# Transposing W_base and the first batch's x1 by 32x32 blocks and a trip through DRAM

## The chip, the cores and the metric

The kernel runs on one core of a Trainium2 chip. The metric is the device time of one execution in microseconds, as the median of several runs. A profiled execution has its own time and its own span, from the first to the last instruction.

The engines are named as in the profile: PE (TensorE, matmuls, with PEld for its weight loads), DVE (VectorE), ACT (ScalarE), POOL (GpSimd) and SP (SyncE, which issues nearly all DMAs here). Each engine works through its own queue in order, and an instruction that waits holds up everything behind it on that engine. That holds for SP too: a DMA that has to wait for data keeps the DMAs behind it from being issued.

## The reference

One transformer layer in float32, with normalisation after each half:

```python
x = layernorm(x + attention(x))        # x: (2, 512, 512)
x = layernorm(x + ffn(x))
```

The attention has 32 query heads over 8 key/value heads of 128, rotary positions and a causal mask. The second half is a linear layer with a low-rank addition, mixed over four experts:

```python
y        = einsum('bth,oh->bto', x, W_base) + b_base      # W_base: (512, 512), o by h
z        = einsum('bth,erh->bter', x, A)                  # A, Bm: 4 active experts of rank 8
contribs = einsum('bter,eor->bteo', z, Bm) * 2.0
alpha    = softmax(log(prior + 1e-12) + (x @ router_W.T + router_b)[..., active])
return y + einsum('bteo,bte->bto', contribs, alpha)
```

Both operands of the first product are contracted over h. TensorE contracts over partitions, so it needs the normalised tokens and W_base with h on the partitions, and both arrive with h along the free dimension. They have to be transposed.

## The kernel before

**Tiles.** The 2 x 512 tokens are eight tiles of 128 tokens, four for each batch (TPB = 4). `x_sb` holds them; the attention's output is added into it, so after the attention it holds x + attention(x). A unit is one key/value head group of one batch; there are 16 units (NU), in four parts each (one part = 128 queries of four heads), so 64 parts.

**Slots.** The middle of the kernel is a hand-written pipeline: `slot(T)` for T from -8 to E + 6, with E = T_END = 256. One slot computes one block of scores (`sc`, 32 queries of four heads). Their masked maximum and exponentials follow in the next slot, and three and four slots later come their normalisation and their 32x32 block transposes. Extra work is put into a slot with `put(slot, f)`; it comes last in that slot's order, in the order of the `put` calls. `A = LAST + LAG_WO` is slot 245, by which the output projection of the first batch has been added, and `T_PROJ` is slot 237.

**The probabilities' way through DRAM.** For `weigh` (`pc<-pT,v`) the probabilities must be transposed as well. VectorE transposes 32x32 blocks into `zt`; `blocks_out` writes them to DRAM (`db`) in four DMAs, one from each group of 32 partitions; `blocks_in` reads them back as `pT` with the blocks in their places. `blocks_out` comes in slots with T % 4 = 3 and `blocks_in` in slots with T % 4 = 1, one part at a time. Both are on the SP queue, as are the loads of wq, wk, wv and wo.

**The first batch's second half.** Its four tiles are `f0`. Each is an `Ffn` object with the steps `stats`, `centre` (normalise in place), `transpose` (four TensorE transposes into PSUM, one ScalarE copy to `xT`, named x1T in the profile), `base` (the main product, eight matmuls of 272 or 276 columns, half of them in each of two slots), `logits`, `alphas`, `low_rank`, `finish` and `add`. They are laid into the slots from A on, while the last parts of the attention of the second batch still run. The `po<-wo,ctxT` matmuls in those slots are its output projection. The second batch's tiles (`fa`, `fb`, `fc`) come after the slots, in plain order.

**W_base.** Four loads of 128 rows are put into slots T_PROJ + 0, 1, 4 and 5. `transposed_base(c)` in slots T_PROJ + 3, 6, 8 and 9 transposes one of them: four TensorE transposes into a bank of PSUM and a ScalarE copy into `wbT`.

**Memory.** The pools open and close in a stack. `late` is a small pool that lives from slot 20 to T_PROJ; it holds `wt_late`, which is used by one set of output weights from slot 197 on. `ffn_pool` opens at T_PROJ in place of the projections' pool. The program's DMAs on the SP queue use eight completion semaphores ("lanes") in turn; a DMA that takes a lane waits until the DMA that had it before has landed, unless that is already known.

Of the kernel before, what the change touches and what calls it, by code (L numbers as in the profile page):

```python
# [9 lines left out]
F32 = mybir.dt.float32  # L10
# [5 lines left out]
P = 128  # L16
# [13 lines left out]
def postln_layer_kernel(  # L30
# [33 lines left out]
    nc = tc.nc  # L64
    B, S, HID = x.shape
    NT = B * S // P
    TPB = S // P
    KC = HID // P
    E_TOT, RK, _ = lora_A.shape
    O = W_base.shape[0]  # L70
    OC = O // P
# [4 lines left out]
    BLK = 32  # L76
    QB = P // BLK
    UNIT = S // BLK
# [17 lines left out]
    def set_units(n):  # L96
        return [u for u in range(NU) if set_of(u) == n]
# [9 lines left out]
    ps_k = ctx.enter_context(tc.tile_pool(name="ps_k", bufs=1, space=bass.MemoryType.PSUM))  # L107
# [3 lines left out]
    dram = ctx.enter_context(tc.tile_pool(name="dram", bufs=2, space=bass.MemoryType.DRAM))  # L111
# [42 lines left out]
    def load_q(n, k):  # L154
        wq_g = wts.tile([P, KC, 2 * D], F32, tag="wq_g", name=f"wq_{n}_{k}", bufs=3)
        lo = (sets[n] * R + 2 * k) * D
        nc.sync.dma_start(out=wq_g, in_=Wq[:, lo : lo + 2 * D].rearrange("(c p) n -> p c n", p=P))
        wqk["q", n, k] = wq_g
# [16 lines left out]
    for n in range(2):  # L175
# [6 lines left out]
        out=tri, in_=tri, pattern=[[-BLK, QB], [-1, BLK]], compare_op=ALU.is_ge,  # L182
# [98 lines left out]
    def transpose_token_tile(dst, src, pool, tag, copy, chunks=range(KC)):  # L281

        tp = pool.tile([P, len(chunks), P], F32, tag=tag, name="tp")
        for n, c in enumerate(chunks):
            nc.tensor.transpose(tp[:, n, :], src[:, ts(c, P)], ident)  # L285
        copy(dst[:, chunks[0] : chunks[-1] + 1, :], tp)

    b_jar = setup.tile([P, BJ, EA, RK], F32, name="b_jar")

# [340 lines left out]
    wt = {}  # L630
# [3 lines left out]
    def wo_block(n, c_half, n_half):  # L634
        return wos[n][:, CH * c_half : CH * (c_half + 1), ts(n_half, NHALF)]

    def wo_sums(n, step):

        if step == 0:
            shape = [P, 3, CH, NHALF]  # L640
            if n == NSETS - 4:
                wt[n] = late["pool"].tile(shape, F32, name="wt_late")
            else:
                wt[n] = wow.tile(shape, F32, tag="wt", name=f"wt_{n}", bufs=1)
        t1, t2, t4 = (wt[n][:, m] for m in range(3))
        b11, b12, b21, b22 = (wo_block(n, c_half, n_half) for c_half in range(2) for n_half in range(2))
        nc.vector.tensor_tensor(
            *((t1, b12, b11), (t2, b22, t1), (b12, b22, b12), (t4, b21, t2))[step], ALU.subtract)
# [104 lines left out]
    class Ffn:  # L753
# [22 lines left out]
        def transpose(self, pool, tag):  # L776
            transpose_token_tile(self.xT, self.x, pool, tag, nc.scalar.copy)
# [107 lines left out]
    def put(slot, f):  # L885
        extra.setdefault(slot, []).append(f)
# [21 lines left out]
    def q_from(u, k):  # L908

        return UNIT * u - 25 + 8 * k  # L910

    pairs = [(n, k) for n in range(NSETS) for k in range(R // 2)]
    for m, (n, k) in enumerate(pairs):
        if n:
            put(q_from(set_units(n)[0], k) - (5 if n == 1 else 9), lambda n=n, k=k: w_sums(n, k))
        if m > 3:
            before, k_before = pairs[m - 3]
            put(q_from(set_units(before)[-1], k_before) + 10, lambda n=n, k=k: load_q(n, k))


    PLAIN_K = 2 * B
    KV_FROM = 8
    late = {}
    PERIOD = VG * B * UNIT
    for p in range(1, G // VG):
        at = PERIOD * p
# [22 lines left out]
    for n in range(NSETS - 2):  # L949
        at = {0: (-5, -4, -3, -2), NSETS - 4: (-16, -15, -15, -13), NSETS - 3: (-11, -9, -6, -5)}.get(n, (0, 1, 1, 3))  # L950
        for k in range(4):
            put(wo_from(set_units(n)[0]) + at[k], lambda n=n, k=k: wo_sums(n, k))
# [98 lines left out]
    for t in range(TPB):  # L1051
        x_to = xT[:, :, ts(t, P)], x_sb[:, t, :]
        if t > 1:
            for c in range(KC):
                k_tile(0, t - 2, c)
        if t < TPB - 1:
            transpose_token_tile(*x_to, *spare[t], copies[t % 2])
        else:
            for n, bank in enumerate((spare[t], (ps_q, "qx"))):
                transpose_token_tile(*x_to, *bank, copies[n], range(2 * n, 2 * n + 2))  # L1060
        if t == 2:
            tb = ps_sc.tile([P, NBIAS], F32, tag="sc", name="tb")
            nc.tensor.transpose(tb, bqk, ident[:NBIAS, :NBIAS])
            nc.vector.tensor_copy(bqkT, tb)
# [63 lines left out]
    T_PROJ = T_END - 19  # L1128
# [1 line left out]
        slot(T)  # L1130
    proj_stack.close()
    ffn_pool = ctx.enter_context(tc.tile_pool(name="ffn", bufs=1))
    wb_sb = ffn_pool.tile([P, OC, HID], F32, name="wb_sb")
    wbT = ffn_pool.tile([P, KC, 2, WX_COLS], F32, name="wbT")
    nc.gpsimd.tensor_copy(wbT[:, :, 0, OH : OH + ARH], arT[:, :, :ARH])
    nc.gpsimd.tensor_copy(wbT[:, :, 1, OH:], arT[:, :, ARH:])
# [5 lines left out]
    QX, QY, SC, CTX = (ps_q, "qx"), (ps_q, "qy"), (ps_sc, "sc"), (ps_ctx, "ctx")  # L1142

    def tiles(ts_, banks, name):
        n = len(ts_)
        norms = Norm(ffn_pool, n, f"a{name}"), Norm(ffn_pool, n, f"f{name}")
        return [Ffn(t, bank, *norms, i) for i, (t, bank) in enumerate(zip(ts_, banks))]

    f0 = tiles(range(TPB), ((QX, QY), (QX, QY), (SC, SC), (QX, QY)), "0")
    fa = tiles([TPB + i for i in order[:2]], ((SC, SC), (WX, WY)), "1a")  # L1150
    (fb,) = tiles([TPB + order[2]], ((QX, QY),), "1b")
# [2 lines left out]
    A = LAST + LAG_WO  # L1154

    def transposed_base(c):
        transpose_token_tile(wbT[:, :, c // 2, ts(c % 2, P)], wb_sb[:, c, :], ps_k, "k", nc.scalar.copy)

    for c in range(OC):
        put(T_PROJ + (0, 1, 4, 5)[c], lambda c=c: nc.sync.dma_start(out=wb_sb[:, c, :], in_=W_base[ts(c, P), :]))  # L1160
        put(T_PROJ + (3, 6, 8, 9)[c], lambda c=c: transposed_base(c))
    put(A - 5, lambda: f0[0].norm1.newton(0, 2))
    for k, f in enumerate(f0):
        put(A + (-7, -6, 0, 0)[k], f.stats)
        if k == TPB - 1:
            put(A, lambda: f0[0].norm1.newton(2, TPB))
        put(A + 1 + k // 2, f.centre)
        put(A + 3 + k // 2, lambda f=f, k=k: f.transpose(*(QX, QY)[k % 2]))
    for f, at in zip(f0, (A + 5, A + 11, A + 13)):
        last = f is f0[2]  # L1170
        for c in range(KC):
            put(at + c // 2, lambda f=f, c=c: f.base(c))
        put(at + 2, lambda f=f: (f.logits(), f.alphas()))
        put(at + 3 + last, f.low_rank)
        if not last:
            put(at + 4, lambda f=f: (f.finish(), f.add()))
# [143 lines left out]
```

## Time and profile before

| | |
|---|---|
| Median of 3 runs | 817.26 us (816.86 to 817.88) |
| The profiled execution: its time / its span | 816.9 us / 815.1 us |
| Granted TensorE clock, mean | 0.998 |
| PE busy | 807.0 us, 3457 matmuls |
| DVE busy | 609.8 us, 1978 instructions |
| ACT busy | 384.9 us, 1074 instructions |
| POOL busy | 338.6 us, 392 instructions |
| Moved by DMA | 116.00 MB, mean 142 GB/s |

The profile's times count from the first instruction of the profiled execution. Each row of a timeline has a start, a length, an engine, the line of the program, the operation, what it writes and reads, and how many instructions it merges. A length includes a pipeline's latency, so that neighbouring rows overlap; the cost of a group of matmuls is read from start to start. Every float32 matmul of the program is two MATMUL records in the profile. Rows of waits give the waiting engine and line, what ended the wait, the total, how often, and the longest.

### The profile page before, as it was taken

To read this page: it belongs to the slowest core of one execution; us is meant where nothing else is said; L and a number is where in the kernel's file an instruction comes from. 1 tells how busy PE (TensorE), PEld (TensorE's weight loads), DVE (VectorE), ACT (ScalarE), POOL (GpSimd) and SP (SyncE) were. 2 spreads that over 40 slices of the span, in tenths; PEclk is the share of its full clock that TensorE was granted. 3 is DMA by queue.
4 is the path that set the end of the run, shared out by engine and by line. 5 is a ranking of instruction groups with operands and counts; after the bars stand their busy time and mean duration, and the time that the engine had idled before them with its cause. 6 is when DMAs were issued, how large, how long until landed. Compare 5 with 4: busy or idle time off the path is not lost.

```text
span 815.1 us, 11389 instructions
## 1 busy us (share of the span) xinstructions
PE 807.0 (99%) x3457; PEld 609.7 (75%) x3457; DVE 609.8 (75%) x1978; ACT 384.9 (47%) x1074; POOL 338.6 (42%) x392
## 2 busy tenths in 40 slices
PE   9999999999999999999999999999999999999996
PEld 7887777777777778777777778777777878656575
DVE  4778877687879886787867876787888689973455
ACT  2355454444545454545435454544545454663244
POOL 8666645421444345322443245343464333420033
PEclk9999999999999999999999999999999999999999
DMA  9025736355455637264544637365453726674211
GB/s 298 26 72 143 219 83 202 91 130 156 134 169 136 182 93 219 77 181 129 147 147 121 178 82 219 91 160 179 137 146 91 232 66 181 189 263 143 77 39 65
DMA packets 84415, 116.00 MB, mean 142 GB/s; under 512 B 6525, under 2 KB 64237, under 8 KB 82306
## 3 DMA queue, kind: packets, MB, share of 16 engines
q1 hardware_dynamic: 83154, 114.71, 49.0%
q8 instruction: 27, 0.44, 0.2%
q10 hardware_dynamic: 752, 0.42, 0.2%
q14 instruction: 34, 0.28, 0.1%
q0 software_dynamic: 448, 0.14, 0.1%
HBM read 71.21 MB, written 44.04 MB: 141 GB/s over the span
## 4 chain that ended last, share of the span: by engine, by line
PE 96%; POOL 1%; DVE 1%; ACT 1%; issue 0%; POOLq 0%
PE pc L618 17%; PE sc L562 15%; PE qx L450 14%; PE wx L450 12%; PE qy L450 10%; PE wy L450 9%; PE kx L450 4%; PE vx L528 4%; PE po L694 3%; PE py L788 3%; PE pv L348 3%; PE pp L365 1%; PE tp L285 1%; PE py L829 1%; POOL zt L191 0%; POOL act_er L220 0%
## 5 line engine op out<-in xcount | busy, mean ns | idle before, releaser
L577 ACT ACTIVATE p<-sc,nmax 128x288 f32<-128x288 f32 (+15 forms) x256 | 124.2, 485 | 197.7 <-DVE nmax L570 175.2
L570 DVE CUSTOM_DVE_ANT_0 sc<-sc,maskw 128x288 f32<-128x288 f32 (+15 forms) x256 | 114.2, 446 | 136.3 <-PE sc L562 134.7
L618 PE MATMUL pc<-pT,v 128*128 128x512 f32 x320 | 165.3, 599 | 0.0
L562 PE MATMUL sc<-kT,qT 128*128 128x160 f32 (+15 forms) x512 | 161.7, 398 | 0.3 <-ACT p L577 0.3
L386 POOL TENSOR_TENSOR qT<-q,t 128x512 f32<-128x512 f32 x64 | 88.0, 1376 | 176.1 <-DVE q L385 165.0
L585 ACT ACTIVATE p<-p,den 128x288 f32<-128x288 f32 (+15 forms) x256 | 133.2, 521 | 0.0
L562 PEld LDWEIGHTS sc<-kT,qT 128*128 128x128 f32 x512 | 96.1, 190 | 21.9 <-issue 8.1
L625 ACT ACTIVATE ctxT<-pc,bqkT 128x512 f32<-128x512 f32 x64 | 44.0, 688 | 114.8 <-PE pc L618 114.7
L437 POOL TENSOR_TENSOR cs<-ctxT 128x256 f32<-128x256 f32 x28 | 22.4, 801 | 158.5 <-PE wy L450 95.4
L593 DVE STREAM_TRANSPOSE zt<-p 128x128 f32<-128x128 f32 (+2 forms) x192 | 81.7, 426 | 0.0
L486 ACT COPY q<-qx 128x256 f32<-128x256 f32 x128 | 47.4, 370 | 51.4 <-PE qx L450 49.8
L618 PEld LDWEIGHTS pc<-pT,v 128*128 128x128 f32 x320 | 57.1, 190 | 18.7 <-issue 5.7
L450 PE MATMUL qx<-xs,wq 128*128 128x256 f32 x256 | 66.3, 381 | 0.0
L450 PEld LDWEIGHTS qx<-xs,wq 128*128 128x128 f32 x256 | 47.3, 190 | 23.2 <-issue 18.4
L595 DVE STREAM_TRANSPOSE zt<-p 128x32 f32<-128x32 f32 (+3 forms) x256 | 57.6, 225 | 0.0
L450 PE MATMUL wx<-wo,ctxT 128*128 128x256 f32 x224 | 57.5, 379 | 0.0
L378 DVE SCALAR_TENSOR_TENSOR t<-q,bqkT,rope_sb 64x512 f32<-64x512 f32 x64 | 52.3, 818 | 3.5 <-ACT q L486 1.7
L381 DVE SCALAR_TENSOR_TENSOR t<-q,bqkT,rope_sb 64x512 f32<-64x512 f32 x64 | 50.3, 786 | 1.5
L577 ACT ACTIVATION_READ_ACCUMULATOR p<-sc,nmax 128x1 f32 x256 | 49.8, 194 | 0.0
L385 DVE SCALAR_TENSOR_TENSOR q<-q,bqkT,rope_sb 128x512 f32<-128x512 f32 x64 | 48.1, 751 | 0.1
L450 PEld LDWEIGHTS wx<-wo,ctxT 128*128 128x128 f32 x224 | 42.5, 190 | 7.0 <-issue 1.4
L680 DVE TENSOR_TENSOR x_sb<-wx,x_sb 128x256 f32<-128x256 f32 x112 | 47.0, 420 | 0.0
(234 smaller groups left out, 1468.3 us busy)
## 6 DMA issues: line engine op xcount, KB each, us to landing
db<-zt SPq DMA_DIRECT2D x64, 256.0 KB, 4.3
pT<-db SPq DMA_DIRECT2D x16, 1024.0 KB, 4.8
db<-zt SPq DMA_DIRECT2D x64, 192.0 KB, 3.3
pT<-db SPq DMA_DIRECT2D x16, 768.0 KB, 4.4
wq<-in_L_attn_Wq_dram SPq DMA_DIRECT2D x20, 512.0 KB, 5.1
wo<-in_L_attn_Wo_dram SPq DMA_DIRECT2D x10, 1024.0 KB, 9.0
db<-zt SPq DMA_DIRECT2D x64, 128.0 KB, 2.4
pT<-db SPq DMA_DIRECT2D x16, 512.0 KB, 4.2
```

Of the source, the lines that this page charges most:

```text
L378: nc.vector.scalar_tensor_tensor(t2[lo, :], q[hi, :], b_ap[hi, :], rope_sb[hi, 1, :], ALU.add, ALU.mult)
L381: nc.vector.scalar_tensor_tensor(t2[hi, :], q[lo, :], b_ap[lo, :], rope_sb[lo, 1, :], ALU.add, ALU.mult)
L385: nc.vector.scalar_tensor_tensor(t1, q, b_ap, rope_sb[:, 0, :], ALU.add, ALU.mult)
L386: nc.gpsimd.tensor_tensor(dst, t1[:, :].rearrange("p (n s) -> p n s", s=BLK), t2[:, :].rearrange("p (n s) -> p n s", s=BLK), ALU.add)
L450: nc.tensor.matmul(ps, lhsT=wt[:, c, :], rhs=xt[:, c, :], start=start and c == 0, stop=c == CH - 1, skip_group_check=True)
L562: nc.tensor.matmul(sc[s][:, :w], lhsT=qT[u][:, i * QB + n].rearrange("p r s -> p (r s)"), rhs=kT[u][:].rearrange("p n s -> p (n s)")[:, :w ...
L570: nc.vector.tensor_tensor_reduce(sc[s][:, :w], sc[s][:, :w], maskw[:, S - w :], -SCALE, -MASKED, ALU.add, ALU.min, nmax[s])
L577: nc.scalar.activation(ptile[s][:, :w], sc[s][:, :w], AF.Exp, bias=nmax[s], scale=-1.0, accum_out=rden[s])
L585: nc.scalar.activation(ptile[s][:, :w], ptile[s][:, :w], AF.Copy, scale=rden[s])
L593: nc.vector.transpose(z[:, :, last - i : last, n, :].rearrange("p q j s -> p j q s"), ptile[s][:, : i * P])
L595: nc.vector.transpose(z[:, : n + 1, last, n, :], ptile[s][:, i * P : w])
L618: nc.tensor.matmul(psc[p], lhsT=v_sb[g // VG, b][:, j, ts(g % VG, D)], rhs=pT[p][:, :, ts(j, P)], start=(j == 0), stop=(j == i))
```

## The change

W_base and the first batch's normalised tokens no longer go through TensorE for their transposition. They go the way of the probabilities: VectorE transposes 32x32 blocks, four DMAs write them to DRAM, one DMA reads them back in the other order, and ScalarE copies them into the layout that the matmuls read.

- For W_base this happens in the middle of the kernel: for each block c of 128 rows, the load in slot 63 + 32c, the block transposes in slot 69 + 32c and the four writes in slot 71 + 32c, through a buffer that shares its place with `wt_late`. It is read back by two DMAs in slots T_PROJ and T_PROJ + 4, and copied to `wbT` in the same slots as before.
- For x1, centring and block transposes of the four tiles come in slots A to A + 3 (centring was in A + 1 and A + 2). The writes of the first two tiles are put into slot A + 2 and of the other two into A + 4, each read back two slots later. The copies to `xT` are in slots A + 5 and A + 9 (the TensorE transposes were in A + 3 and A + 4). The first `base` starts in slot A + 6 instead of A + 5; the other two keep their slots.

The second batch's tiles are transposed on TensorE as before.

```diff
+    def blocks_of(z, src):
+        nc.vector.transpose(z.rearrange("p q c s -> p c q s"), src)
+
+    def blocks_to(rows, z):
+        for a in range(QB):
+            nc.sync.dma_start(out=rows[:, :, a, :].rearrange("q t x -> t q x"), in_=z[ts(a, BLK)])
...
             if n == NSETS - 4:
-                wt[n] = late["pool"].tile(shape, F32, name="wt_late")
+                wt[n] = late["pool"].tile(shape, F32, tag="wt_late", name="wt_late")
...
+    wb_rows = dram.tile([QB, BLK, OC, QB, HID // QB], F32, name="wb_rows", bufs=1)
+    wb_tmp = {}
+
+    def base_blocks(c, step):
+        if step == 0:
+            wb_tmp[c] = late["pool"].tile([P, 3, HID], F32, tag="wt_late", name=f"wb_{c}")
+            nc.sync.dma_start(out=wb_tmp[c][:, 0, :], in_=W_base[ts(c, P), :])
+            return
+        z = wb_tmp[c][:, 1, :]
+        if step == 1:
+            blocks_of(z.rearrange("p (q k s) -> p q k s", k=KC, s=BLK), wb_tmp[c][:, 0, :])
+        else:
+            blocks_to(wb_rows[:, :, c], z.rearrange("p (q x) -> p q x", q=QB))
+
+    for c in range(OC):
+        for step, at in enumerate((-6, 0, 2)):
+            put(2 * UNIT * c + 69 + at, lambda c=c, step=step: base_blocks(c, step))
...
-    wb_sb = ffn_pool.tile([P, OC, HID], F32, name="wb_sb")
+    wb_sb = ffn_pool.tile([P, OC, QB, KC, BLK], F32, name="wb_sb")
...
+    x1_z = [ffn_pool.tile([P, QB, 2, KC, BLK], F32, name=f"x1_z_{n}") for n in range(2)]
+    x1_rows = [dram.tile([QB, BLK, QB, 2 * HID // QB], F32, name=f"x1_rows_{n}", bufs=1) for n in range(2)]
+    x1_in = [ffn_pool.tile([P, QB, 2, KC, BLK], F32, name=f"x1_in_{n}") for n in range(2)]
+
+    def x1_out(n):
+        blocks_to(x1_rows[n], x1_z[n][:].rearrange("p q i c s -> p q (i c s)"))
+
+    def x1_back(n):
+        nc.sync.dma_start(
+            out=x1_in[n][:].rearrange("p a i c s -> p a (i c s)"), in_=x1_rows[n][:].rearrange("q t a x -> (q t) a x"))
+
+    def x1_chunks(k):
+        nc.scalar.copy(
+            f0[k].xT[:].rearrange("p c (a s) -> p c a s", s=BLK), x1_in[k // 2][:, :, k % 2].rearrange("p a c s -> p c a s"))
...
     def transposed_base(c):
-        transpose_token_tile(wbT[:, :, c // 2, ts(c % 2, P)], wb_sb[:, c, :], ps_k, "k", nc.scalar.copy)
-
+        nc.scalar.copy(
+            wbT[:, :, c // 2, ts(c % 2, P)].rearrange("p k (a s) -> p k a s", s=BLK),
+            wb_sb[:, c].rearrange("p a k s -> p k a s"))
+
+    for n in range(2):
+        put(T_PROJ + (0, 4)[n], lambda n=n: nc.sync.dma_start(
+            out=wb_sb[:, 2 * n : 2 * n + 2].rearrange("p c a k s -> p c a (k s)"),
+            in_=wb_rows[:, :, 2 * n : 2 * n + 2].rearrange("q t c a x -> (q t) c a x")))
     for c in range(OC):
-        put(T_PROJ + (0, 1, 4, 5)[c], lambda c=c: nc.sync.dma_start(out=wb_sb[:, c, :], in_=W_base[ts(c, P), :]))
         put(T_PROJ + (3, 6, 8, 9)[c], lambda c=c: transposed_base(c))
     put(A - 5, lambda: f0[0].norm1.newton(0, 2))
     for k, f in enumerate(f0):
         put(A + (-7, -6, 0, 0)[k], f.stats)
         if k == TPB - 1:
             put(A, lambda: f0[0].norm1.newton(2, TPB))
-        put(A + 1 + k // 2, f.centre)
-        put(A + 3 + k // 2, lambda f=f, k=k: f.transpose(*(QX, QY)[k % 2]))
-    for f, at in zip(f0, (A + 5, A + 11, A + 13)):
+        at = A + (0, 1, 2, 3)[k]
+        put(at, f.centre)
+        put(at, lambda f=f, k=k: blocks_of(x1_z[k // 2][:, :, k % 2], f.x))
+    for n, at in enumerate((A + 2, A + 4)):
+        put(at, lambda n=n: x1_out(n))
+        put(at + 2, lambda n=n: x1_back(n))
+    for k in range(TPB):
+        put(A + (5, 5, 9, 9)[k], lambda k=k: x1_chunks(k))
+    for f, at in zip(f0, (A + 6, A + 11, A + 13)):
```

## The prediction

> **What bounds the kernel now.** I read the page's shares first, then the chain, then TensorE's waits, and only then the last 90 us instruction by instruction. The first two lines are the page's busy row and its chain.
>
> ```profile
> PE 807.0 (99%) x3457; PEld 609.7 (75%) x3457; DVE 609.8 (75%) x1978; ACT 384.9 (47%) x1074; POOL 338.6 (42%) x392
> PE 96%; POOL 1%; DVE 1%; ACT 1%; issue 0%; POOLq 0%
> ```
>
> TensorE is busy from end to end and the chain runs through it. From 26 us to 790 us its waits hold one entry, 0.35 us. So every matmul that is taken out is worth its time, and every wait of TensorE that is put in costs its length. The transposes that go, from the tile view of `tp`, and their place, from the timeline:
>
> ```profile
> L285 PE MATMUL tp<-ident,wb_sb x16: 272/273/273, 711.1 to 725.3; 128*128 128x128 f32 x16
> ...
> 729.80 1.10 PE L618 MATMUL pc<-pT,v 128*128 128x512 f32 x2
> 730.74 1.04 PE L285 MATMUL tp<-ident,x_sb 128*128 128x128 f32 x8
> 731.61 1.88 PE L694 MATMUL po<-wo,ctxT 128*128 128x512 f32 x4
> ...
> 734.41 1.04 PE L285 MATMUL tp<-ident,x_sb 128*128 128x128 f32 x8
> 735.29 1.88 PE L694 MATMUL po<-wo,ctxT 128*128 128x512 f32 x4
> 737.00 0.36 PE L562 MATMUL sc<-kT,qT 128*128 128x96 f32 x2
> 737.20 1.05 PE L618 MATMUL pc<-pT,v 128*128 128x512 f32 x2
> 738.09 2.01 PE L788 MATMUL py<-wbT,x1T 128*128 128x272 f32 x8
> ```
>
> Starts count, not the 273 ns (they overlap): eight transposes take 0.87 us (730.74 to 731.61). At 738.09 the first tile's feed-forward matmul (`base`) starts. Next the SP queue there, in which the new round trip has to fit, and what it waits for:
>
> ```profile
> 723.24 0.34 SPq L611 DMA_DIRECT2D pT<-db  x1
> 723.67 0.40 SPq L162 DMA_DIRECT2D wo<-in_L_attn_Wo_dram  x1
> 725.79 1.81 SPq L603 DMA_DIRECT2D db<-zt  x4
> 734.65 0.34 SPq L611 DMA_DIRECT2D pT<-db  x1
> 738.44 2.84 SPq L603 DMA_DIRECT2D db<-zt  x4
> ...
> SPq L611 <- DMA db<-zt: 21.7, 13, 6.9
> ```
>
> The `pT` issue at 734.65 stood 6.9 us behind the `db` writes issued from 725.79 to 727.60. Those lay behind 1 MB of `pT` and 1 MB of `wo`. The stretches (last columns: granted clock, DMA share, GB/s) show the engines full until about 733.6:
>
> ```profile
> 732.00:733.00 1.00, 1.00 (x4) 0.48 (x3) 0.00 (x0) 1.00 (x3) 0.00 (x0) 1.00 1.07 396
> 733.00:734.00 1.00, 1.00 (x6) 0.52 (x5) 0.47 (x1) 0.31 (x3) 0.00 (x0) 1.00 0.58 211
> 734.00:735.00 1.00, 1.00 (x8) 0.71 (x7) 1.00 (x6) 0.00 (x0) 0.00 (x0) 1.00 0.00 2
> 739.00:742.00 3.00, 3.00 (x12) 1.87 (x11) 0.15 (x1) 0.00 (x0) 0.00 (x0) 1.00 0.90 180
> ```
>
> **Part 1, removed.** Starts give 0.44, 0.43, 0.43 and 0.43 us for the four W_base groups (711.13, 716.64, 721.11, 724.93), and 0.87 and 0.88 for the two x1 groups: 3.48 us of TensorE. If nothing new waits, this is all won. In slots 240 to 243 VectorE is nearly full (2.93 of 3 us in 710 to 713), so up to 0.9 us might stay there; I take 0.
>
> **Part 2, W_base in mid-kernel** (slots 63 to 167). Added: 4 loads of 256 KB, 4 block transposes of 128x512, 16 writes of 64 KB.
>
> ```profile
> L593 DVE STREAM_TRANSPOSE zt<-p 128x384 f32<-128x384 f32 x64 | 35.7, 559 | 0.0
> L585 ACT ACTIVATE p<-p,den 128x512 f32<-128x512 f32 x16 | 11.4, 712 | 0.0
> db<-zt SPq DMA_DIRECT2D x64, 128.0 KB, 2.4
> pT<-db SPq DMA_DIRECT2D x16, 512.0 KB, 4.2
> ```
>
> By the slope from 256 (426 ns) to 384 (559) a 128x512 transpose takes about 0.69 us. It lies at slot 69 (227.8 us), where VectorE idles 1.4 and 2.0 us for scores. The writes (4 x 0.44 us of SP) stand between `db` (232.68 to 234.44) and its `pT` (235.80). They hold that issue to 236.2 and put 256 KB, 1.3 us at about 200 GB/s, in front: `pT` lands near 241 instead of 239, and its first `pc` is at 247.43. The wq and wk loads behind it move as little. The W_base load at slot 63 falls into the 2.7 us in which `pT` waits for `db` anyway. Cost 0. Without that cover each write group would cost up to 1.7 us, 7 in all.
>
> **Part 3, W_base back.** Two 512 KB loads in slots 237 and 241 replace four of 256 KB, at the same SP places. The first lands by 706.95 + 4.2 = 711.2, and ScalarE copies at 711.8. The four copies read SBUF (712 ns row) instead of PSUM (586 ns): +0.13 us each beside an engine at 47%. Cost 0; a late first load could hold ScalarE, and scores behind it, by up to 0.5.
>
> **Part 4, x1 through DRAM.** The step that decides. Without waits the first `base` moves one slot on and starts at: slot 245 at 719.50 - 0.87 = 718.63, then score, `pc`, `po` as now: 3.33, 3.39, 2.58, 2.80, 2.80, 2.81, and 1.08 for slot 251's score and `pc`: 737.4. In the old order the same work would be done 3.48 us later, so a first `base` at 737.4 + 3.5 = 740.9 gives the old end: each us beyond is lost, each us before is won.
>
> VectorE: centre and transpose of tiles 0 and 1 come into slots 245 and 246 (0.5 + 0.6 us pitch each). Following its queue from the score of slot 244 (ready 718.0), the transposes for `db` end at 726.3 (725.8 now), the fourth x1 tile at 730.4, and slot 247's mask at 728.6 against 729.4 now. No score is late.
>
> SP and the transfers, in SP's new order `wo`, `db` x4, x1 write x4, `pT`, x1 read:
> 1. `db` is issued 726.4 to 728.2 and three x1 writes to 729.5. The fourth uses a completion lane that `wo` holds (landing 8.5 us, about 732.2), so it goes out near 732.
> 2. `db` data end about 733.2 (everything before is 0.4 earlier without two transpose groups). The 512 KB of x1 follow at 400 GB/s (the row at 732) to 200 (the row at 739, writes from 32 partitions): 1.3 to 2.6 us, 734.5 to 735.8. Completion follows about 1 us later, as now (733.6 to 734.65): 735.5 to 736.8.
> 3. `pT` (768 KB) is issued near 734.3 and read until 737.6. The x1 read, issued 735.9 to 737.2, lands 4.2 us later by its row or behind `pT`: 739.8 to 741.4.
> 4. A ScalarE copy, 0.7 us: `base` at 740.5 to 742.1; I take 741.0.
>
> TensorE would stand at 737.4 and wait 3.6 us: 3.6 - 3.5 = +0.1 us. Queued behind the x1 read on SP are the second x1 writes, `db` of the next part (738.44 now, about 739 then) and its `pT`. That one lands about 752 and its first `pc` is due at 755 (754.68 now), so 3 us are left. Behind the x1 copies ScalarE holds the normalise of slot 248 and the exp of slot 250, whose score buffer TensorE needs one `base` half (1.85 us) later; it just fits, at most 0.5.
>
> [...] Here the granted clock is 0.998 and no gap after the start passes 0.4 us, so no run yet shows it. [...] I take 0 and keep 1.7 for the range.
>
> **Sum.** -3.5 removed, 0 mid-kernel, +3.6 waiting: +0.1 us on the profiled execution (span 815.1, whole 816.9), so 817.0 there. That execution is 0.36 under the median 817.26, so I predict 817.4.
>
> **The rivals.**
> - *The round trip is hidden.* The x1 writes slip between the `wo` packets and the read lands by 738.5: wait 0 to 1.5 us, -3.5 to -2.0, time 813.8 to 815.3. For: three of four writes are issued 4 us before they are due, and reads and writes together reach 400 GB/s. Against: the 6.9 us wait, which shows this queue full just then. Chance 0.2.
> - *The read comes late and the clock falls.* One mechanism: SP issues in order, so the x1 read waits for the fourth write, that one for `wo`, and the read lies behind `pT`. From a `base` at 742.5 on it is slower; at 743 the wait is 5.6 us, +2.1, and a halved clock makes it +3.8: 819.4 to 821.1. For: `wo` at 8.5 us is the longest transfer here. Against: `wo` ends before `db` does, which is waited for anyway. Chance 0.35.
> - *The change does not take the work away.* Excluded: the order of instructions has 32 transposes fewer on TensorE. That nothing at all moves the end is excluded by the 99%.
>
> **How the numbers follow.** The likeliest case (0.45): the wait eats the gain, 815.7 to 818.8, time 817.4. A measurement of this kernel tells about 0.2% (1.6 us) from no change: the chances are 0.2 faster, 0.45 within, 0.35 slower. The range reaches half into the hidden case and most of the late one: 814.6 to 820.6.
>
> **What would show it.** TensorE's waits should have a new entry near 737 of 3 to 4 us at `base`, released by ScalarE's x1 copy, that copy by the x1 read. SP should show the fourth x1 write behind `wo` and the read after 735. `tp` should have 32 fewer matmuls, and no new wait before 700 us. Wrong if `base` starts without a wait (faster), if a wait shows in mid-kernel or at the second half's `pT`, or if the clock row falls after the wait.

## The result and the profile after

The kernel after takes 821.95 us (median of 6 runs, 820.17 to 822.55), the kernel before beside it 817.28 us (6 runs, 816.86 to 817.88). The ratio is 1.0054, with a 95% interval of 1.0044 to 1.0065: 4 to 5 us slower, where 817.4 us (814.6 to 820.6) was predicted. The profiled execution took 822.55 us, span 820.8 us, 5.7 us more than the span before.

The work did leave TensorE: 3425 matmuls instead of 3457. The page's busy row and its chain, then TensorE's waits from 26 to 816 us (waiting line, what ended the wait, total us, times, longest):

```profile
PE 807.6 (98%) x3425; PEld 607.8 (74%) x3425; DVE 615.2 (75%) x1986; ACT 384.9 (47%) x1074; POOL 337.3 (41%) x392
PE 96%; POOL 1%; issue 1%; DVE 1%; DMA 1%; ACT 0%; POOLq 0%
...
PE py L798 <- issue: 4.8, 1, 4.8
PE pc L628 <- DMA pT<-db: 0.6, 1, 0.6
PE wx L460 <- DVE x_sb L690: 0.2, 1, 0.2
```

32 matmuls fewer, and yet 0.6 us more busy. One wait of 4.8 us is new, at the first `base` (L798). Both have their place in TensorE's timeline, here after and then before:

```profile
718.66 1.12 PE L628 MATMUL pc<-pT,v 128*128 128x512 f32 x2 [0.61 <-DMA pT<-db]
...
737.65 1.02 PE L628 MATMUL pc<-pT,v 128*128 128x512 f32 x2
743.50 3.99 PE L798 MATMUL py<-wbT,x1T 128*128 128x272 f32 x8 [4.83 <-issue]
747.29 0.74 PE L572 MATMUL sc<-kT,qT 128*128 128x160 f32 x2
747.82 1.88 PE L628 MATMUL pc<-pT,v 128*128 128x512 f32 x2
749.53 2.02 PE L798 MATMUL py<-wbT,x1T 128*128 128x272 f32 x8
```

```profile
718.64 1.02 PE L618 MATMUL pc<-pT,v 128*128 128x512 f32 x2
...
739.93 1.88 PE L694 MATMUL po<-wo,ctxT 128*128 128x512 f32 x4
...
742.73 2.01 PE L788 MATMUL py<-wbT,x1T 128*128 128x272 f32 x8
```

The `pc` of 737.65 ends about 0.86 us after its start (the usual time from one `pc` to the next matmul), so TensorE reaches the `base` at 738.5. It starts at 743.50, 5.0 us later, when the first of the two x1 copies has ended (743.4). The row of waits names no releaser here; in e3 and e14 below it names this copy. The first half of the `base` then takes 3.79 us from start to start (743.50 to 747.29), where the second half takes 1.86 (749.53 to the next row at 751.39) and the same half took 1.84 before (738.09 to 739.93). The granted clock says why (stretches: length, TensorE's busy time, clock, DMA share, GB/s):

```profile
741.00:742.00 1.00, 0.00 (x0) 1.00 1.00 356
742.00:743.00 1.00, 0.00 (x0) 0.86 1.07 388
743.00:744.00 1.00, 0.50 (x1) 0.50 1.06 378
...
746.00:747.00 1.00, 1.00 (x4) 0.50 0.77 252
...
749.00:750.00 1.00, 1.00 (x4) 0.73 0.76 311
750.00:751.00 1.00, 1.00 (x6) 1.00 1.07 451
```

Reading 0.86 and 0.73 as a switch between 1.00 and 0.50 within the row, the clock is halved from about 742.7 to 749.5: 6.8 us. The `base`'s input came late by this chain, SP's issues first (merged: x4 is four DMAs, the length is that of the group), then its one long wait on a lane, then ScalarE:

```profile
724.77 0.43 SPq L162 DMA_DIRECT2D wo<-in_L_attn_Wo_dram  x1
726.50 1.82 SPq L613 DMA_DIRECT2D db<-zt  x4
728.36 5.23 SPq L296 DMA_DIRECT2D x_rows<-x_z  x4
735.56 0.34 SPq L621 DMA_DIRECT2D pT<-db  x1
736.82 0.34 SPq L1186 DMA_DIRECT2D x_in<-x_rows  x1
...
SPq L296 <- DMA wo<-in_L_attn_Wo_dram: 2.4, 1, 2.4
...
742.78 1.14 ACT L1190 COPY x1T<-x_in 128x512 f32<-128x512 f32 x2 [9.42 <-DMA x_in<-x_rows]
```

The fourth x1 write, the eighth DMA issued after `wo`, waits 2.4 us for it to land, the `pT` transfer goes out in front of the x1 read, and the read lands 5.9 us after its issue. Up to the last 130 us the two traces run alike: the score of 224 columns (`sc` 128x224) is at 690.47 us before and at 690.42 after, with W_base's new work in mid-kernel already done.

**The difference as a sum.** Had TensorE simply done the old order with nothing new, the `pc` that ends at 738.5 after would have ended at 740.9: before, the second half of the `base` starts at 742.73, and the first half of 1.84 us, which lies ahead of it there, is still to come in the new order. So 2.4 us were gained by then, of 3.48. The wait cost 5.0. From the first half of the `base` to the second, 6.03 us pass at the lower clock (743.50 to 749.53) against 3.05 us in the run below that keeps its clock: 3.0. Together -2.4 + 5.0 + 3.0 = +5.6 us, for +5.7 measured on the spans.

### The profile page after: what moved, and what is told of

The parts are those of the page before. It is cut to its first block, busy times and chain, and to the rows that moved or that the text cites. A ratio compares the mean times of both kernels' runs of the same rounds, so it can differ in the third digit from the quotient of the medians.

```text
span 820.8 us, 11374 instructions
## 1 busy us (share of the span) xinstructions
PE 807.6 (98%) x3425; PEld 607.8 (74%) x3425; DVE 615.2 (75%) x1986; ACT 384.9 (47%) x1074; POOL 337.3 (41%) x392
## 4 chain that ended last, share of the span: by engine, by line
PE 96%; POOL 1%; issue 1%; DVE 1%; DMA 1%; ACT 0%; POOLq 0%
PE pc L628 17%; PE sc L572 15%; PE qx L460 13%; PE wx L460 12%; PE qy L460 10%; PE wy L460 9%; PE kx L460 4%; PE vx L538 4%; PE po L704 3%; PE py L798 3%; PE pv L358 3%; PE pp L375 1%; PE py L839 1%; DMA pT<-db 1%; PE tp L285 0%
```

## The experiments

Each kernel is the kernel after with the edit shown, unless the text says otherwise. A stands for slot 245. Medians are compared through their ratios to the kernel before, which ran beside each. The traces differ by up to 1.25 us at the score of 224 columns near 690 us (690.26 to 691.51), and by as much already at a score of 288 columns near 99 us (98.83 to 100.08), ahead of every edit. So stretches within one trace are compared, counted from that score where two traces must be set side by side.

**e1_warm: fill the wait.** Ten matmuls, whose result is not used, keep TensorE busy until the `base`.

```diff
+    def warm():
+        tp = ps_q.tile([P, 2 * P], F32, tag="qx", name="warm")
+        for _ in range(10):
+            nc.tensor.matmul(tp, lhsT=rope_sb[:, 0, :P], rhs=rope_sb[:, 0, : 2 * P], start=True, stop=True)
+
+    put(A + 6, warm)
```

> The changed kernel, with ten matmuls of 128x256 (0.43 us each, 4.3 us in all, results not used) put in front of the first base, where TensorE waited 5.0 us for the x1 read; nothing else is changed. Theory (the wait, and then a halved clock on top of it): the matmuls fit into the wait, base still starts near 743.5, the granted clock stays 1.00 from 742 to 749 where it was 0.50, and the 3.3 us that the work after the wait took longer are gone: 818.7 us. Rival (the lower clock is only a record, or the end is set by another engine): about 822 as before the matmuls. A third way, the matmuls are simply added: 822 + 4.3 = 826.

820.03 us (819.25 to 820.45), ratio 1.0031 (1.0019 to 1.0043). In the timeline the base starts as late as ever, but at full speed:

```profile
739.45 4.48 PE L1227 MATMUL warm<-rope_sb 128*128 128x256 f32 x20
744.39 2.08 PE L798 MATMUL py<-wbT,x1T 128*128 128x272 f32 x8 [0.46 <-ACT x1T L1190]
746.31 0.43 PE L572 MATMUL sc<-kT,qT 128*128 128x160 f32 x2
...
747.44 2.01 PE L798 MATMUL py<-wbT,x1T 128*128 128x272 f32 x8
```

739.45 to 744.39 is the same 4.9 us, and from the first half of the `base` to the second it takes 3.05 us. The clock stays at 1.00, so the slow stretch was the clock's doing. In medians 1.9 us are back, not the 3.3 that were expected: in two of the six runs of the kernel after the mean clock was 0.997 instead of 0.994, so not every run loses the full 3.0 us.

**e14_warm3: leave 3.6 us of the wait.** The same with `range(3)`. This is the length that the prediction took.

> As e1, with three matmuls of 128x256 in front of the base instead of ten: TensorE is busy 1.3 us longer and then waits 3.6 us instead of 5.0, the length that the prediction took; the base starts at the same time. Theory A (3.6 us is short enough): granted clock 1.00, 820.0 us as e1. Theory B (it is not): the clock halves as after a wait of 5.0 us, and the time is 821.5 to 822 us, as after.

821.42 us (819.74 to 822.86), ratio 1.0044 (1.003 to 1.0057). TensorE waits 3.8 us, and the clock falls all the same:

```profile
738.77 1.46 PE L1227 MATMUL warm<-rope_sb 128*128 128x256 f32 x6
744.03 3.99 PE L798 MATMUL py<-wbT,x1T 128*128 128x272 f32 x8 [3.80 <-ACT x1T L1190]
...
742.00:743.00 1.00, 0.00 (x0) 0.88 1.07 384
743.00:744.00 1.00, 0.00 (x0) 0.50 1.08 377
...
749.00:750.00 1.00, 1.00 (x3) 0.71 0.82 344
```

Again 6.8 us at half. One of its five runs (819.74 us) kept a mean clock of 1.000; the other four took 820.96 to 822.86 us at 0.994 to 0.997. So here the loss was usual, not certain, and a wait of the predicted 3.6 us would most likely not have been free of it.

**e3_x1_only and e2_w_only: one half of the change each.** In e3 W_base is loaded and transposed as before; in e2 W_base takes the new way, and x1 is transposed on TensorE in the old slots with the old first `base`. Each edit restores lines of the diff above:

```diff
e3:
...
+        transpose_token_tile(wbT[:, :, c // 2, ts(c % 2, P)], wb_sb[:, c, :], ps_k, "k", nc.scalar.copy)
...
e2:
...
+        put(A + 1 + k // 2, f.centre)
+        put(A + 3 + k // 2, lambda f=f, k=k: f.transpose(*(QX, QY)[k % 2]))
+    for f, at in zip(f0, (A + 5, A + 11, A + 13)):
```

> x1 alone goes through VectorE and DRAM; W_base is loaded and transposed on TensorE as in the kernel before. Theory (the first base starts when the x1 read has landed, whatever lies in front): base within 1 us of 743.5 again, and since the W_base transposes lie in front of the wait they only shorten it, from 5.0 to 3.5 to 4.2 us. The total is then 821 to 822 if the clock still halves, and near 818.7 if the shorter wait leaves it alone. Rival (the two parts add up): the changed kernel plus what W_base alone gains, 822.9 or more.

> W_base alone goes through VectorE and DRAM; x1 is transposed on TensorE in its old slots. Theory: the mid-kernel part costs nothing, 1.74 us of transposes go, but the pT of part 58 lands at 718.6 whatever TensorE does, so that the 0.87 us of the first two groups are waited away: 1.74 - 0.87 = 0.9 us faster, 816.4 us, with a wait of about 0.6 us at pc near 718. Rival (all of it is won): 815.5. Rival (mid-kernel transfers and VectorE work cost time): 817.3 or more, with new waits before 700 us.

e3: 822.19 us (820.56 to 823.64), ratio 1.0056 (1.0042 to 1.0069), with a wait of 4.7 us at the `base` and the halved clock. e2: 817.23 us (816.35 to 817.89), ratio 0.9998 (0.999 to 1.0006); 816.4 was expected. All of the loss belongs to x1, and W_base's 1.73 us bring nothing that can be measured. The trace of e2 shows who took them (TensorE's waits after 26 us):

```profile
PE pc L628 <- DMA pT<-db: 0.9, 2, 0.5
```

Counted from the score of 224 columns, e2 stands 0.33 us ahead of before at the score of 384 columns (716.43 - 691.34 = 25.09 against 25.42), 0.77 ahead at the score of 416 columns, and only 0.19 ahead at the `pc` behind it, which waits for `pT`. That `pT` is issued 23.8 us after the score in e2 and 23.9 us in the kernel before; TensorE only reaches it sooner. At 730 us a second wait for `pT` takes another 0.7 (both measured from start to start; the row counts 0.9 for the two), and at the first `base` 0.3 us are left (47.33 against 47.62).

**e5_wo_later: take `wo` from in front of the x1 writes.**

```diff
-    for n in range(2, NSETS):
+    for n in range(2, NSETS - 1):
         put(wo_from(set_units(n - 2)[-1] + 1) + 1, lambda n=n: load_wo(n))
...
+    put(A + 4, lambda: load_wo(NSETS - 1))
```

> The last load of wo (1 MB) moved from in front of the first x1 writes to behind the second ones, nothing else. Theory A (the read of x1 is late because wo stands in front of its writes, by its transfer and by the fourth write's wait of 2.4 us): the fourth x1 write goes out about 2.4 us earlier, the read of x1 lands near 740 instead of 742.7, the wait of TensorE falls from 5.0 to about 2.3 us, the granted clock stays at 1.00, and the time is about 817.3 us (816 to 818.5). Theory B (what holds the read is the P transfers themselves, db and pT, which stand on the same queue): the wait stays over 4 us, the clock still halves, 820 to 822 us.

817.38 us (816.38 to 818.14), ratio 1.0000 (0.9991 to 1.0008): the time of theory A, with a shorter wait than the 2.3 us that it had. SP's issues and the copy:

```profile
730.25 3.05 SPq L296 DMA_DIRECT2D x_rows<-x_z  x4
733.66 0.34 SPq L621 DMA_DIRECT2D pT<-db  x1
735.63 0.34 SPq L1186 DMA_DIRECT2D x_in<-x_rows  x1
...
741.23 1.14 ACT L1190 COPY x1T<-x_in 128x512 f32<-128x512 f32 x2 [6.14 <-DMA x_in<-x_rows]
```

The read goes out 44.12 us after the score of 224 columns, against 46.40 in the kernel after: 2.3 us earlier, the length of the lane wait. TensorE's wait at the `base` is 1.5 us, and the clock stays at 1.00. But the read still takes 5.6 us.

**e12_read_first: the read in front of `pT`.** e5 with one more edit:

```diff
-        put(at + 2, lambda n=n: x1_back(n))
+        put(at + 2 - (n == 0), lambda n=n: x1_back(n))
```

> e5 with one line of SP's order changed: the first read of x1 goes out before the pT transfer of part 60 instead of behind it. Theory A (the read lands 5.6 us after its issue in e5 because 768 KB of pT stand in front of it): it lands about 4 us after its issue, near 739.5 on e5's axis, the wait of 1.5 us is gone, pT is not waited for since its first pc comes after the base: about 816.0 us. Theory B (its landing is what 512 KB take under the traffic of this stretch, whatever the order): the read still takes over 5 us, the wait stays over 1 us, 817.4 us or more.

816.17 us (814.66 to 816.55), ratio 0.9982 (0.9975 to 0.999).

```profile
734.93 0.34 SPq L1186 DMA_DIRECT2D x_in<-x_rows  x1
735.43 0.34 SPq L621 DMA_DIRECT2D pT<-db  x1
...
738.59 1.14 ACT L1190 COPY x1T<-x_in 128x512 f32<-128x512 f32 x2 [3.41 <-DMA x_in<-x_rows]
739.47 1.02 PE L628 MATMUL pc<-pT,v 128*128 128x512 f32 x2
740.33 2.01 PE L798 MATMUL py<-wbT,x1T 128*128 128x272 f32 x8
```

From issue to copy 3.7 us instead of 5.6: 768 KB of `pT` stood in front. The `base` follows its `pc` without a gap, and `pT` is not missed. What remains are two waits for earlier `pT`, 1.9 us in all.

**e11_second_later: the second round trip two slots later** (from e5), and **e15_first_and_later**, the same from e12.

```diff
-    for n, at in enumerate((A + 2, A + 4)):
+    for n, at in enumerate((A + 2, A + 6)):
...
-        put(A + (5, 5, 9, 9)[k], lambda k=k: x1_chunks(k))
+        put(A + (5, 5, 11, 11)[k], lambda k=k: x1_chunks(k))
```

> e5 with the second x1 round trip two slots later, so that wo and db follow the first read instead of the x1 writes. Theory A (what is issued behind the read does not slow it): landing, wait and first base as in e5, but db and pT of part 61 are earlier: 817.4 us or up to 0.5 less. Theory B (the 512 KB of writes issued just behind the read take its bandwidth): it lands about 1 us earlier, 816.5 us.

> e12 (read of x1 in front of pT) with e11's later second round trip. If both effects add: no wait at the base, pT of part 61 earlier, about 815.8 us (e12 816.17 less the 0.4 us between e5 and e11). If the first base no longer waits in e12, e11's part has nothing left to save there: 816.2 us.

e11: 816.98 us (815.96 to 818.89), ratio 0.9999 (0.999 to 1.0007). In its one trace the read takes 4.7 us (735.20 to 739.87) instead of 5.6, as theory B has it, and the wait is 0.8 us; but its ratio is e5's, so what this is worth is not shown. e15: 815.75 us (814.46 to 816.31), ratio 0.9977 (0.9968 to 0.9986). It is the fastest of all, 1.8 us faster than the kernel before beside it. Its interval overlaps that of e12, so that the two edits add is likely and not proved.

**e4_late_base and e8_both: move the first `base` instead.** e4 delays it by two slots; e8 does that and takes `wo` away as in e5.

```diff
-        put(A + (5, 5, 9, 9)[k], lambda k=k: x1_chunks(k))
-    for f, at in zip(f0, (A + 6, A + 11, A + 13)):
+        put(A + (7, 7, 9, 9)[k], lambda k=k: x1_chunks(k))
+    for f, at in zip(f0, (A + 8, A + 13, A + 13)):
```

> The changed kernel, with the first base put two slots later (A + 8), the x1 copies of its tiles on ScalarE two slots later too (A + 7), and the second tile's base at A + 13 instead of A + 11; the transfers are untouched. Theory (the transfers set when base can start, and only the work in front was too short): 4.0 us of other matmuls (1.13 and 2.91) now come before base, which starts near 743.5 after a wait of about 1 us and without a lower clock: 817.3 - 3.5 + 1.0 (waited away before slot 245) + 1.0 = 815.8 us, faster than the kernel before. Rival (the loss is in contention of the transfers or in VectorE, not in the place of base): within 1 us of 822.

> wo moved as in e5, and the first feed-forward tiles two slots later as in e4 (slots A+8, A+13, A+13, their copies at A+7). If e4's 818.3 us was pT of parts 60 and 61 landing behind wo, both its waits of 1.8 and 2.2 us shrink to under 1 us each: about 816 us. If they come from ScalarE standing 4.0 us at the x1 copy with the softmax work behind it, and from the x1 transfers themselves in front of db and pT, the time stays near 818 us.

e4: 818.29 us (815.62 to 820.19), ratio 1.0007 (0.9999 to 1.0015); 815.8 was expected, a miss. The profiled execution is the slowest of its 13. In it the wait at the `base` is gone and four waits for `pT` stand in its place:

```profile
PE pc L628 <- DMA pT<-db: 5.1, 4, 2.2
...
745.14 1.14 ACT L1190 COPY x1T<-x_in 128x512 f32<-128x512 f32 x2 [4.02 <-DMA x_in<-x_rows]
746.19 0.37 ACT L595 ACTIVATE p<-p,den 128x96 f32<-128x96 f32 x1
```

ScalarE stands 4.0 us at the x1 copy with the probabilities' normalisation behind it, and one `pT` takes 8.0 us to land (749.07 to 757.1). e8: 817.48 us (815.53 to 818.51), ratio 0.9998 (0.9989 to 1.0006); 816 was expected. Its one profiled execution has few waits (1.5 us) and took 816.6 us, but the median of 13 runs does not follow it, so its trace does not explain it.

**e9_pool_copy: the copies on GpSimd** (e8 with `nc.gpsimd.tensor_copy` in `x1_chunks`).

> e8 with the four x1 copies on GpSimd, which has nothing to do there, instead of ScalarE. If the x1 copy at the head of ScalarE's queue holds the exp and the normalise behind it, and so db and pT, this is 1 to 2 us faster than e8. If only the transfers count, it is equal to e8 within 0.5 us, or slower where a GpSimd copy takes longer than the 0.61 us on ScalarE.

817.38 us (816.06 to 818.26), ratio 1.0000 (0.9992 to 1.0008), equal to e8. With `wo` out of the way, ScalarE's place in the queue is not what holds e8.

**e6_half, e10_pair2_only, e13_three: send only what has time.** e6 transposes tiles 0 and 1 on TensorE in the old slots and sends tiles 2 and 3 through DRAM. e10 does that without W_base's new way. e13 sends tile 1 as well, three tiles in one round trip.

```diff
-        at = A + (0, 1, 2, 3)[k]
-        put(at, f.centre)
-        put(at, lambda f=f, k=k: blocks_of(x1_z[k // 2][:, :, k % 2], f.x))
+        put(A + 1 + k // 2, f.centre)
+        if k < 2:
+            put(A + 3, lambda f=f, k=k: f.transpose(*(QX, QY)[k]))
+        else:
+            put(A + 2, lambda f=f, k=k: blocks_of(x1_z[1][:, :, k % 2], f.x))
+            put(A + 9, lambda k=k: x1_chunks(k))
+    put(A + 4, lambda: x1_out(1))
+    put(A + 6, lambda: x1_back(1))
...
+    for f, at in zip(f0, (A + 5, A + 11, A + 13)):
```

> Tiles 0 and 1 of x1 transposed on TensorE in the old slots, with the first base in its old slot A+5; only tiles 2 and 3, whose base comes from slot A+13 on (tile 2) or after the loop (tile 3), and W_base go through DRAM. Theory (the round trip costs only where a base waits for it): no wait at any base, no lower clock, and one TensorE group of 0.88 us less than e2_w_only: about 816.4 us. Rival (the x1 transfers cost through db and pT, which stand behind them on SP): pT of part 61 lands late and is waited for, 817.5 us or more.

> The kernel before with tiles 2 and 3 of x1 alone through DRAM: W_base and tiles 0 and 1 stay on TensorE. Theory (a transpose group is worth its 0.88 us where its reader comes late, and W_base through DRAM is worth only what its waits leave, 0.3 us): about 816.5 us, and e6 (816.13 us) differs from it by W_base alone. Rival (W_base made e6's gain): 817.3 us.

> e6 with tile 1 too through DRAM, in one round trip with tiles 2 and 3 (192 KB for each write, 768 KB for the read); only tile 0, whose base comes first, stays on TensorE. Its base starts in slot A+11, near 755 us, so the read (landing near 749) is in time. Theory: another 0.44 us less of TensorE and no wait: 815.7 us. Rival (the larger transfers delay db and pT of part 61, which stand between them): equal to e6 or slower, 816.1 to 817 us.

e6: 816.13 us (815.01 to 817.24), ratio 0.9986 (0.998 to 0.9993). e10: 816.44 us (815.53 to 817.1), ratio 0.9985 (0.9979 to 0.9992). One x1 group is worth its time where nobody waits for the read: in e6 it lands at 747.6 and tile 2's `base` comes at 762. W_base adds nothing to it. e13: 817.77 us (816.92 to 818.3), ratio 1.0005 (0.9997 to 1.0014). This is the rival's side, and beyond its 817 us: by the ratios 1.6 us slower than e6. The profiled execution, the fastest of its 13, shows in part why:

```profile
PE po L704 <- ACT ctxT L635: 1.2, 1, 1.2
...
743.58 1.01 SPq L1186 DMA_DIRECT2D x_in<-x_rows  x1
...
750.22 1.66 ACT L1190 COPY x1T<-x_in 128x512 f32<-128x512 f32 x3 [1.95 <-DMA x_in<-x_rows]
751.78 0.68 ACT L635 ACTIVATE ctxT<-pc,bqkT 128x512 f32<-128x512 f32 x1
```

The 768 KB read takes 6.6 us where e6's 512 KB took 4.6, ScalarE waits 1.95 us for it and then copies three tiles, and the context copy behind them keeps a `po` waiting 1.2 us.

## Why the prediction was wrong, point by point

**The cause was right, and so was its place.** The wait at the first `base`, released by the x1 copy, that by the read; the fourth write behind `wo`; the read behind `pT`; a second `pT` (issued 747.29, landing 5.2 us later) that is not waited for: all as written. Mid-kernel cost nothing: from the score of 288 columns near 99 us to that of 224 near 690 it is 591.43 us before and 591.42 after. What came true as a whole is the second rival, the late read with the falling clock, 0.9 us beyond its 821.1. Three terms of the sum were mis-sized.

1. *Part 1, "up to 0.9 us might stay there; I take 0".* All of it stayed, though `pT` held it and not VectorE, for which it was named: the `pc` at 718.66 stands where before's stood (718.64), with 0.61 us of waiting for `pT`. Of 3.48 us, 2.4 were there at the `base`. TensorE reached it at 738.5 instead of 737.4. For W_base alone, e2 and the pair e6 and e10 put the value at nothing. So the full count of a removed matmul needs that what it waits for next is early, and here `pT` was not.
2. *Part 4, steps 2 and 3: "everything before is 0.4 earlier", and "lands 4.2 us later".* `pT` of part 59 went out at 724.38 (723.24 before), and `wo` behind it at 724.77 instead of 723.67. The change is hardly the cause: `pT` goes out 34.0 us after the score of 224 columns here, 33.9 in e3 and 34.4 in e10, which load W_base as before and have no new transfer up to there, and 32.8 in the one trace of before. Why that trace was early is not shown. With a landing of 8.5 us that puts the fourth write at 733.3, not 732. The read still went out within the range given, at 736.82. It then took 5.9 us where 4.2 was added. The 4.2 is the median of sixteen `pT` reads of 512 KB, not the time of a read behind 768 KB. With that out of its way (e12) the read took 3.7 us. The second bound (behind `pT`, 741.4) was the right one, and still 1.3 us short. Copy included, the `base` came at 743.5 against 740.5 to 742.1, and the wait was 5.0 against 3.6 us.
3. *The clock, "I take 0 and keep 1.7 for the range".* It cost 3.0 us in the profiled execution and 1.9 us in the medians (e1). The 1.7 us was the author's estimate, which no trace had shown, and a fall of the clock was set aside, since "no run yet shows it". But the trace of before shows one behind its last matmul (rows below). e14 shows it for a wait in front of matmuls: at 3.8 us the clock falls; at 1.5 us (e5) and at 1.8 and 2.2 us (e4) it does not. The estimate was too small as well: the low clock lasted 6.8 us, and 3.0 us were lost.

The rows of before that bear on the third term, its last matmul and two stretches behind it:

```profile
808.35 0.59 PE L853 MATMUL ph<-bmT,zT 128*128 128x256 f32 x2
...
811.00:812.00 1.00, 0.00 (x0) 0.69 0.41 156
812.00:813.00 1.00, 0.00 (x0) 0.50 0.65 235
```

TensorE ends at 808.9, and from 811.4 on the clock is halved, 2.4 us later. The 3.7 us at half up to the end of the span are all that the prediction's 0.998 lacks to 1. So a row stood against taking 0 for a wait of 3.6 us.

With these terms the prediction's own sum reads -2.4 + 5.0 + 3.0 instead of -3.5 + 3.6 + 0, +5.6 instead of +0.1 us.

**Where the expected gain went,** in medians: the clock 1.9 us (e1), `wo` in front of the writes a further 2.5 (e5), `pT` in front of the read 1.5 (e12), each a ratio against the kernel before. With the last two mended and the second pair later (e15), 815.75 us are left, 1.8 of the 3.48 us.

## What to carry to other kernels

Count a removed matmul only up to the next thing that TensorE waits for: find when that lands, and take the smaller of the two. When a step goes through DRAM on a shared queue, list what stands in front of each leg, and add what its bytes and its completion wait cost to the leg (here 1.9 us for 768 KB of `pT`, from e5 to e12, and 2.4 us for `wo`). The same change went from 0.5% slower to 0.2% faster by moving one load and one issue.

A wait put into a TensorE that never waited can cost more than its length: in the five falls set out below the clock halved 2.4 to 4.2 us after TensorE had gone idle, while a wait of 2.2 us in e4 left it at 1.00. If the forecast wait is of that size, the clock's loss (1.9 us in the medians here) belongs in the sum and not only in the range. A kernel without a gap in its work still has its end, where its own trace can show a fall of the clock, as before did 2.4 us behind its last matmul.

## What the runs showed of the hardware beyond this

The clock did not fall at a fixed time after TensorE went idle: 4.2 us after in the kernel after (738.5 to 742.7) and 2.9 at its end (814.9 to 817.8), 3.2 in e3 (740.0 to 743.3), 2.5 in e14 (740.2 to 742.8), 2.4 at the end of the kernel before (808.9 to 811.4). It then stayed low for 6.8 us in all three traces in which it fell in front of the `base`, though TensorE worked again after 0.8 us of that in the kernel after, 1.6 in e3 and 1.3 in e14.

A wait of 2.2 us left the clock at 1.00, that of e4 for `pT` from 754.9 to 757.1 (stretches as above):

```profile
754.00:755.00 1.00, 0.89 (x3) 1.00 0.26 67
755.00:756.00 1.00, 0.00 (x0) 1.00 0.06 25
756.00:757.00 1.00, 0.00 (x0) 1.00 0.06 24
757.00:758.00 1.00, 0.89 (x2) 1.00 0.03 9
```

What sets the moment of the fall, and why one run of e14 kept a mean clock of 1.000, is not shown.

The new VectorE transposes of 128x512 took 671 (W_base) and 711 ns (x1), where 0.69 us was estimated, and the ScalarE copies 612 to 614 ns, where 712 was taken: no part of the loss.
